# Four edits to a state-space scan that runs beside an attention layer: engine order, pairs of tokens, pairs of channels, and one broadcast load per unit

## The chip, the cores and the metric

The kernel runs on one core of a Trainium2 chip. A core has a matrix engine (PE, with its weight loads shown as PEld), a vector engine (DVE), an activation engine (ACT), a general engine (POOL) and a queue engine (SP) that here issues all the transfers. Sixteen DMA engines move the data. Work tiles lie in SBUF (128 partitions); PE writes to PSUM. Each engine runs its own list of instructions in order and waits on semaphores for the others.

The metric is device microseconds of one execution. Before the change the median of three runs was 19929.43 us (19923.0 to 19977.06).

## The reference

A batch of 16 images of 256 channels and 1024 tokens goes through two residual layers. The first is group norm, attention with 4 heads, and a feed-forward block. The second is group norm and a selective state-space scan with 512 channels `d` and 64 states `n`. The scan is what matters here:

```
delta = softplus(dt @ dt_proj_w.T + dt_proj_b)
A = -exp(A_log)

def step(h, inp):
    d_t, B_t, C_t, u_t = inp
    dA = exp(d_t[..., None] * A)
    h = dA * h + (d_t * u_t)[..., None] * B_t[:, None, :]
    y = einsum('bdn,bn->bd', h, C_t)
    return (h, y)

y = ys.transpose(1, 0, 2) + u * D
y = y * silu(z)
return (y @ out_proj_w.T) * ctx
```

For every image there are 512 x 64 recurrences over 1024 tokens, and each token's 64 states are then multiplied by `C` and summed.

## The kernel before

**Units.** The scan is cut into 4096 units: 16 images (`b`), 4 blocks of 128 channels (`k`), 4 blocks of 256 tokens (`t`), 2 halves of the channel block (`h`), 8 units (`i`) in a half. A unit holds 8 channels: each of its four scans carries two channels (`j`), 64 states each, on 128 partitions, for 256 tokens. The four scans of a unit are numbered by `r` and `e`.

**One unit's path.**
- `load` (L668) has SP bring delta times u of the 8 channels from the DRAM tile `dus` into a buffer `dub` of 128 partitions by 4 x 256 (L695): two transfers of 256 KB, each a row of 4 KB copied to 64 partitions. There are five such buffers (`dutp`, L84), and a unit's load stands in the text four units ahead.
- `inputs` (L700) multiplies the buffer by `B` on POOL, in two instructions (L705).
- `decay` (L707) spreads delta, kept as three bf16 pieces, over the partitions with four matmuls into two PSUM tiles `a` of four (L715), and ACT takes the exponential in place, four instructions (L721).
- `scan` (L723) runs four scans on DVE (L733) into `hbuf`, one buffer for each half.

`load` for the first unit of a token block also brings `pieces`, `bt` and `ct` (L674 to L682); at (h, i) = (1, 4) it brings `u_y` and `z_y`.

**Outputs of a half.** When the eight units of a half are scanned, the generator `outputs` (L749) goes on beside the next half, one `next` per unit. `sums(s)` (L755) forms the products by `C` for 32 tokens: 32 matmuls, each with a 16-column stationary piece of `cd` (the spread `C`, made by `spread_c`, L739) and a 32-column moving piece of `hbuf` (32 slots at one token), in four column groups of PE. Two ACT instructions (L774) sort the result into `y2`, eight matmuls (L780) turn it so that channels lie on partitions, and DVE adds `u * D` (L785); after the second half it multiplies by the gate (L789) and the result is stored.

**Side work.** While an image is scanned, `attention_layer` and `scan_inputs` prepare the next one and `gate_and_store` finishes the previous one. These are generators with 296 and 15 steps, fed into the loop at an even rate, 311 steps over 234 units (L806 to L842). `scan_inputs` stores delta times u into `dus` with eight transfers per block of channels (L611) and the three pieces into `dps` with two (L625).

**Who sets the order.** The text is written in the order of the main loop: `load(n + 4)`, `inputs(n + 2)`, a step of the running outputs, side steps, `scan(n)`, `decay(n + 2)`. A list scheduler of the framework then orders each engine's instructions, by its own estimate of when each could start; it may move an instruction ahead of others in the text.

Of the kernel before, what the change touches and what calls it, by code (L numbers as in the profile page):

```python
# [51 lines left out]
def attention_then_scan_kernel(  # L52
# [25 lines left out]
    wts = pool("wts", 1)  # L78
    wide = pool("wide", 8)
    half = pool("half", 4)  # L80
    pcp = pool("pcp", 2)
    ptp = pool("ptp", 4)
    small = pool("small", 2)
    dutp = pool("dutp", 5)  # L84
# [44 lines left out]

    a_neg = work("a_neg", ND * NS)
    nc.scalar.activation(a_neg, col("A_log", 0, ND * NS), AF.Exp)
    nc.vector.tensor_scalar(a_neg, a_neg, -1.0, None, ALU.mult)
    acol = const.tile([P, DI // 2], F32, name="acol")
    for k in range(ND):
        ps = psum("acol_ps")
        for j in range(2):
            nc.tensor.matmul(
                ps[ts(j, NS), :64], a_neg[:, ts(k, NS)], ident[:, j:P:2], start=True, stop=True  # L140
            )
        nc.scalar.copy(acol[:, ts(k, 64)], ps[:, :64])
    pick = const.tile([96, 16, 2, NS], BF16, name="pick")
    for p in range(3):
        r = ts(p, 32)
        v = ident[r, r].rearrange("p (i j) -> p i j", j=2)
        nc.vector.tensor_copy(pick[r], v.unsqueeze(3).to_broadcast([32, 16, 2, NS]))


    par = const.tile([P, 2], F32, name="par")  # L150
    turn = const.tile([P, 32], F32, name="turn")
    grid = ident.rearrange("p (g r) -> p g r", g=4)
    for j in range(2):
        nc.vector.tensor_reduce(par[:, j : j + 1], grid[:, :, j:16:2], AX.XY, ALU.add)
    nc.vector.tensor_tensor(
        turn.rearrange("p (g c) -> p g c", g=4), grid[:, :, 0:16:2], grid[:, :, 1:16:2], ALU.add
    )

    rel = dram1.tile([C, L], F32, name="rel", tag="rel")
    for k in range(KC):  # L160
# [301 lines left out]
    def scan_inputs(b):  # L462
# [110 lines left out]

        dps = dram.tile([ND * 3 * P, L], BF16, name="dps", tag="dps")
        dus = dram.tile([ND * NT * P, TB], F32, name="dus", tag="dus")
        dpv = dps.rearrange("(k p q) t -> k q p t", p=3, q=P)
        duv = dus.rearrange("(k t h m r) c -> k h r m t c", k=ND, t=NT, h=2, r=4)
        for d in range(ND):
            delta = work("delta")
            pss = []  # L580
            for hf in range(2):
                ps = psum("d_ps")
                nc.tensor.matmul(ps, wdt_s[:, ts(d, P)], dt[:RANK, hs(hf)], start=True, stop=True)
                pss.append(ps)
            yield
            es = [hwork("sp_e") for _ in range(2)]
            for e, ps in zip(es, pss):
                nc.scalar.activation(e, ps, AF.Abs, bias=col("dt_b", d))
                nc.scalar.activation(e, e, AF.Exp, scale=-1.0)
                nc.scalar.activation(ps, ps, AF.Relu, bias=col("dt_b", d))  # L590
            yield
            ss = [hwork("sp_s") for _ in range(2)]
            for s, e in zip(ss, es):
                nc.vector.tensor_scalar(s, e, 1.0, None, ALU.add)
                nc.vector.scalar_tensor_tensor(e, s, 1.0, e, ALU.subtract, ALU.subtract)
            yield
            for s in ss:
                nc.scalar.activation(s, s, AF.Ln)
            yield
            for hf in range(2):  # L600
                nc.vector.tensor_tensor(ss[hf], ss[hf], es[hf], ALU.subtract)
                nc.vector.tensor_tensor(delta[:, hs(hf)], ss[hf], pss[hf], ALU.add)
                yield
            del es, ss, pss
            du = work("du")
            nc.vector.tensor_tensor(du, delta, us[d], ALU.mult)
            yield
            for hh in range(2):
                for r in range(4):
                    at = 64 * hh + 16 * r  # L610
                    nc.sync.dma_start(  # L611
                        duv[d, hh, r], du[at : at + 16].rearrange("m (t c) -> m t c", t=NT)
                    )
            for hf in range(2):
                pc = pcp.tile([P, 3, HL], BF16, name="pc", tag="pc")
                o = delta[:, hs(hf)]
                nc.scalar.copy(pc[:, 0, :], o)
                yield
                nc.vector.tensor_tensor(o, o, pc[:, 0, :], ALU.subtract)
                yield  # L620
                nc.scalar.copy(pc[:, 1, :], o)
                yield
                nc.vector.tensor_tensor(pc[:, 2, :], o, pc[:, 1, :], ALU.subtract)
                yield
                nc.sync.dma_start(dpv[d][:, :, hs(hf)], pc)  # L625
        st.update(zs=zs, gs=gs, ud=ud, rows=rows, dps=dps, dus=dus)
        st["ys"] = dram.tile([DI, L], F32, name="ys", tag="ys")
        yield
# [39 lines left out]
    def load(n):  # L668
        b, k, t, h, i = units[n]
        st = state[b]  # L670
        if (h, i) == (0, 0):
            pieces = blk.tile([96, ND, TB], BF16, name="pieces", tag="pieces")
            for p in range(3):
                nc.sync.dma_start(  # L674
                    pieces[ts(p, 32)],
                    st["dps"][ds((3 * k + p) * P, P), ts(t, TB)].rearrange("(r q) t -> q r t", q=32),
                )
            bt = blk.tile([P, TB], F32, name="bt", tag="bt")
            ct = blk.tile([P, TB], F32, name="ct", tag="ct")
            for j in range(2):  # L680
                nc.sync.dma_start(bt[ts(j, NS)], st["rows"][:NS, ts(t, TB)])
                nc.sync.dma_start(ct[ts(j, NS)], st["rows"][NS:, ts(t, TB)])  # L682
            blocks[b, k, t] = {"pieces": pieces, "bt": bt, "ct": ct}
        if (h, i) == (1, 4):
# [3 lines left out]
            nc.sync.dma_start(z, st["zs"][ts(k, P), ts(t, TB)])  # L688
            blocks[b, k, t].update(u=u, z=z)
        du = dutp.tile([P, 4, TB], F32, name="dub", tag="dub")  # L690
        src = st["dus"].rearrange(
            "(k t h i j r) c -> k t h i j (r c)", k=ND, t=NT, h=2, i=8, j=2
        )[k, t, h, i]
        for j in range(2):
            nc.sync.dma_start(  # L695
                du[ts(j, NS)].rearrange("p r c -> p (r c)"), src[j : j + 1].partition_broadcast(NS)
            )
        loaded[n] = du

    def inputs(n):  # L700
# [6 lines left out]
    def decay(n):  # L707
# [3 lines left out]
        for r in range(2):  # L711
            a = aps.tile([P, 2, TB], F32, name="a", tag="a")
            for e in range(2):
                w = pick[:, 8 * e + i].rearrange("p j n -> p (j n)")
                nc.tensor.matmul(a[:, e, :], w, pieces[:, 2 * h + r, :], start=True, stop=True)  # L715
            decays[n].append(a)
        for r in range(2):
            for e in range(2):
                q = 64 * k + 32 * h + 16 * r + 8 * e + i
                a = decays[n][r][:, e, :]  # L720
                nc.scalar.activation(a, a, AF.Exp, scale=acol[:, q : q + 1])  # L721

    def scan(n):  # L723
# [3 lines left out]
        hbuf = now["h", h]  # L727
        for r in range(2):
            for e in range(2):
                s = 16 * r + 8 * e + i  # L730
                hh = hbuf[:, s, :]
                first = hbuf[:, s, TB - 1 : TB] if t else 0.0
                nc.vector.tensor_tensor_scan(  # L733
# [2 lines left out]
        del decays[n], loaded[n]  # L736


    def spread_c(b, k, t):  # L739
        if (k, t) == (0, 0):  # L740
            now["cd"] = hst.tile([P, TB // 8, P], F32, name="cd", tag="cd")
            nc.gpsimd.memset(now["cd"], 0.0)
        cd = now["cd"]
        ct = blocks[b, k, t]["ct"].rearrange("p (a c) -> p a c", c=8)
        for j in range(2):
            nc.scalar.copy(cd[ts(j, NS), :, j : j + 127 : 18], ct[ts(j, NS)])


    def outputs(b, k, t, h):  # L749
        if (t, h) == (0, 0):  # L750
            now["yb"] = yps.tile([P, HL], F32, name="yb", tag="yb")
            nc.vector.memset(now["yb"][:, :TB], 0.0)
        cd, yb, hbuf = now["cd"], now["yb"], now["h", h]

        def sums(s):  # L755
            for c in range(8):
                for g in range(4):
                    at = 32 * s + 8 * g + c
                    nc.tensor.matmul(  # L759
                        yb[32 * g : 32 * g + 16, ts(s, SLOTS)],  # L760
                        cd[:, at // 8, ts(at % 8, 16)], hbuf[:, :, at],
                        start=(c == 0), stop=(c == 7),
                    )

        for s in range(5):
            sums(s)
            yield
        sums(5)
        sums(6)
        yield  # L770
        sums(7)
        y2 = blk.tile([P, 2 * TB], F32, name="y2", tag="y2")
        for j in range(2):
            nc.scalar.activation(  # L774
                y2[:, j : 2 * TB : 2], yb[:, :TB], AF.Identity, scale=par[:, j : j + 1]
            )
        yield
        own = ts(h, 64)
        for s in range(8):
            nc.tensor.matmul(  # L780
                yb[own, ds(TB + 32 * s, 32)], y2[:, ts(s, 64)], turn, start=True, stop=True
            )
        yield
        u, z = blocks[b, k, t]["u"], blocks[b, k, t]["z"]
        nc.vector.scalar_tensor_tensor(  # L785
            u[own], u[own], col("D", k)[own], yb[own, TB:], ALU.mult, ALU.add
        )
        if h == 1:
            nc.vector.tensor_tensor(u, u, z, ALU.mult)  # L789
# [16 lines left out]
    for n, (b, k, t, h, i) in enumerate(units):  # L806
# [21 lines left out]
        if i == 0 and n > 0:  # L828
            g = outputs(*units[n - 1][:4])
            next(g)  # L830
            running.append(g)
        if (h, i) == (0, 7):
            spread_c(b, k, t)
        if at >= 12:
            due += rate
# [10 lines left out]
        pass  # L846
    for _ in gate_and_store(B - 1):
        pass


# [53 lines left out]
```

## Time and profile before

| | |
|---|---|
| median of 3 runs | 19929.43 us |
| the profiled execution | 19887.59 us |
| its span on the core | 19885.7 us |
| first scan starts, last scan ends | 474.8 us, 19855.4 us |
| DVE busy | 13669.1 us (69%) |
| PE busy | 13574.2 us (68%) |
| POOL busy | 10583.8 us (53%) |
| ACT busy | 10128.3 us (51%) |
| moved by DMA | 2845.56 MB, mean 143 GB/s |
| of that, the `dub` loads | 8192 transfers of 256 KB |

No engine is busy for more than seven tenths of the span, and the busy shares stay much the same from one image to the next. The rows of a profile give, for each group of instructions, the busy time, the mean of one, the idle time of the engine just before them and what ended most of that idle time. DVE and PE work on the scan and on the side work alike, so their sums mix two things; the last image is scanned with nothing left to prepare and shows the scan almost alone.

### The profile page before, as it was taken

The numbers are of one execution on the slowest core, as the hardware profiler recorded it, in microseconds if no ns is written. First come the engines' busy times: TensorE is split into PE (matmuls) and PEld (weight loads), VectorE is DVE, ScalarE is ACT, GpSimd is POOL, SyncE is SP. The second block draws the span as 40 slices with busy tenths as digits, with TensorE's granted clock in tenths as the row PEclk, the third lists the DMA queues.
The fourth block names the chain that finished last, engine by engine and source line by source line (L and its number), as shares of the span: only waits on it lengthen the run. The fifth ranks groups of instructions, "written<-read, shape, count | busy, mean of one in ns | idle before, by whom it ended". The sixth has DMA issues, their size and how long they took to land. (4 is left out here: it accounts for less than half of the span.)

```text
span 19885.7 us, 697095 instructions
## 1 busy us (share of the span) xinstructions
PE 13574.2 (68%) x300176; PEld 8113.6 (41%) x300176; DVE 13669.1 (69%) x20751; ACT 10128.3 (51%) x21923; POOL 10583.8 (53%) x8214
## 2 busy tenths in 40 slices
PE   6866858668586675857758677585765858668555
PEld 2433434344343443434434344343443434434333
DVE  4766767667677676766767767676676767767666
ACT  3554545545455454554545545454554555545544
POOL 0555555555555555555555555555555555555555
PEclk7876868778687786877868778687876868778666
DMA  2555555555555555555555555555555555555555
GB/s 66 134 138 148 148 147 143 141 147 150 145 142 143 144 146 156 143 140 143 149 152 143 142 143 150 148 152 134 143 147 146 151 140 147 147 145 150 147 145 140
DMA packets 1178858, 2845.56 MB, mean 143 GB/s; under 512 B 193872, under 2 KB 571088, under 8 KB 1175760
## 3 DMA queue, kind: packets, MB, share of 16 engines
q1 hardware_dynamic: 1175760, 2800.95, 52.7%
q8 instruction: 2347, 38.45, 0.9%
q14 instruction: 751, 6.15, 0.1%
HBM read 2539.08 MB, written 261.10 MB: 141 GB/s over the span
## 5 line engine op out<-in xcount | busy, mean ns | idle before, releaser
L705 POOL TENSOR_TENSOR dub<-dub,bt 128x512 f32<-128x512 f32 x8192 | 10527.2, 1311 | 8992.9 <-DMA dub<-dus 7682.3
L721 ACT ACTIVATE a<-a,acol 128x256 f32<-128x256 f32 x16384 | 6984.7, 450 | 7445.7 <-PE a L715 7166.1
L733 DVE TENSOR_TENSOR_SCAN h<-a,h,dub 128x256 f32<-128x256 f32 x12288 | 8104.6, 726 | 1151.0 <-issue 610.2
L759 PE MATMUL yb<-h,cd 128*16 128x32 f32 x262144 | 4642.6, 234 | 2477.5 <-issue 2188.6
L715 PE MATMUL a<-pieces,pick 96*128 96x256 bf16 x16384 | 3819.6, 338 | 2960.0 <-DVE h L733 2885.2
L759 PEld LDWEIGHTS yb<-h,cd 128*16 128x16 f32 x262144 | 3925.7, 115 | 3615.6 <-issue 3239.2
L715 PEld LDWEIGHTS <-pick 96*128 96x128 bf16 x16384 | 1563.1, 111 | 5561.8 <-issue 5071.8
L733 DVE TENSOR_TENSOR_SCAN h<-a,dub 128x256 f32<-128x256 f32 x4096 | 2457.2, 666 | 571.5 <-POOL dub L705 342.7
L785 DVE SCALAR_TENSOR_TENSOR u_y<-u_y,vec,yb 64x256 f32<-64x256 f32 x512 | 244.6, 478 | 2211.5 <-PE yb L780 1167.2
L354 PE MATMUL s_ps<-ka,qa 32*128 32x512 f32 x2048 | 1177.8, 917 | 64.8 <-DVE mx L345 60.7
L345 DVE TENSOR_REDUCE mx<-s_ps 128x1 f32<-128x512 f32 x1024 | 664.4, 676 | 514.5 <-PE s_ps L354 511.1
L399 ACT ACTIVATE pt<-st_ps 128x512 f32<-128x512 f32 x1024 | 563.6, 597 | 721.3 <-PE st_ps L397 719.8
L780 PE MATMUL yb<-turn,y 128*64 128x32 f32 x8192 | 691.0, 242 | 269.9 <-ACT y L774 265.7
L780 PEld LDWEIGHTS yb<-turn,y 128*64 128x64 f32 x8192 | 619.6, 158 | 466.2 <-ACT y L774 351.3
L384 PE MATMUL av<-pt,vv 128*64 128x512 f32 x2048 | 701.4, 634 | 98.0 <-ACT pt L399 97.8
L774 ACT ACTIVATE y<-yb,par 128x256 f32<-128x256 f32 x1024 | 467.6, 493 | 530.3 <-PE yb L759 523.3
L397 PE MATMUL st_ps<-qa,ka 33*128 33x512 f32 x2048 | 663.3, 649 | 0.5 <-ACT qa L374 0.5
L354 PEld LDWEIGHTS s_ps<-ka,qa 32*128 32x128 f32 x2048 | 361.9, 251 | 361.6 <-DVE mx L345 291.4
L512 PE MATMUL g_ps<-w,xp 128*128 128x256 f32 x1536 | 419.9, 420 | 0.0
L512 PEld LDWEIGHTS g_ps<-w,xp 128*128 128x128 f32 x1536 | 374.6, 328 | 15.5 <-issue 5.6
L545 DVE SCALAR_TENSOR_TENSOR u<-up,cwh,u 128x1024 f32<-128x1024 f32 x192 | 326.7, 1703 | 31.6 <-ACT u L538 30.2
L397 PEld LDWEIGHTS st_ps<-qa,ka 33*128 33x128 f32 x2048 | 176.2, 187 | 404.3 <-issue 398.5
(126 smaller groups left out, 8106.3 us busy)
## 6 DMA issues: line engine op xcount, KB each, us to landing
dub<-dus SPq DMA_DIRECT2D x8192, 256.0 KB
dps<-pc SPq DMA_DIRECT2D x128, 384.0 KB
pieces<-dps SPq DMA_DIRECT2D x768, 64.0 KB
xs<-in_x_dram SPq DMA_DIRECT2D x64, 512.0 KB
zs<-z SPq DMA_DIRECT2D x64, 512.0 KB
z_y<-zs SPq DMA_DIRECT2D x256, 128.0 KB
ud<-u SPq DMA_DIRECT2D x64, 512.0 KB
u_y<-ud SPq DMA_DIRECT2D x256, 128.0 KB
```

The lines of the kernel that those rows point to most:

```text
L345: nc.vector.tensor_reduce(mx[:, e, c, hf : hf + 1], s, AX.X, ALU.max)
L354: nc.tensor.matmul(s, qa[r, ts(c, P)], ka[r, hs(hf)], start=True, stop=True)
L384: nc.tensor.matmul(av[ts(e, 2 * DH)], vv[j // (NJ // 2)][:, j % (NJ // 2), 2 * pair + e, :], pts[e], start=(j == 0), stop=(j == NJ - 1),)
L397: nc.tensor.matmul(s, ka[r, ts(j, P)], qa[r, hs(hf)], start=True, stop=True)
L399: nc.scalar.activation(pt, s, AF.Exp)
L512: nc.tensor.matmul(ps[:, ts(q, C)], xp[k][:, ds(first + t, P, 4)], wg_s[:, k, t, :], start=(i == 0), stop=(i == 3 * KC - 1),)
L705: nc.gpsimd.tensor_tensor(v, v, bt, ALU.mult)
L715: nc.tensor.matmul(a[:, e, :], w, pieces[:, 2 * h + r, :], start=True, stop=True)
L721: nc.scalar.activation(a, a, AF.Exp, scale=acol[:, q : q + 1])
L733: nc.vector.tensor_tensor_scan(hh, decays[n][r][:, e, :], loaded[n][:, 2 * r + e, :], first, ALU.mult, ALU.add)
L759: nc.tensor.matmul(yb[32 * g : 32 * g + 16, ts(s, SLOTS)], cd[:, at // 8, ts(at % 8, 16)], hbuf[:, :, at], start=(c == 0), stop=(c == 7),)
L780: nc.tensor.matmul(yb[own, ds(TB + 32 * s, 32)], y2[:, ts(s, 64)], turn, start=True, stop=True)
```

## The change

- **Order.** At the end of the text, every instruction of PE, ACT, DVE and POOL is made to follow the one before it on its engine in the text, for the scheduler only (no semaphore comes of it). SP is not among the four.
- **Two tokens at once.** A product by `C` takes `hbuf[:, :, at : at + 2]`, 64 moving columns. `sums` has 16 matmuls instead of 32. The stationary pieces of `cd` give four rows for each of 4 pairs of tokens in place of two rows for each of 8 tokens, and half of what a matmul writes is not wanted. One ACT copy takes the 512 columns to `y2`, and 32 turning matmuls, in pairs that add into PSUM, pick the wanted rows by four masks (`turn`, 128 x 4 x 32). The steps of `outputs` are spread differently: two `sums` in each of the first four, then the turn, then DVE. `spread_c` is called at (h, i) = (0, 5) instead of (0, 7).
- **Pairs 32 apart.** The two channels of one scan are 32 apart instead of neighbours, and slots are numbered 4 i + 2 r + e. The columns of `acol`, the masks `pick` and the layouts of `dps` and `dus` follow. `dus` is stored with one transfer per block of channels instead of eight, `dps` with eight of 16 partitions by 3 x 2 KB instead of two of 128 by 3 x 1 KB, `pieces` loaded with one instead of three. `pcp` has one buffer of double length.
- **One load.** A unit's `dub` comes with one transfer of 512 KB: two rows of 4 KB, each copied to 64 partitions.

```
-    pcp = pool("pcp", 2)
+    pcp = pool("pcp", 1)
...
-    par = const.tile([P, 2], F32, name="par")
-    turn = const.tile([P, 32], F32, name="turn")
+    turn = const.tile([P, 4, 32], F32, name="turn")
+    nc.vector.memset(turn, 0.0)
     grid = ident.rearrange("p (g r) -> p g r", g=4)
...
+    for e in range(2):
+        for j in range(2):
+            v = turn[:, 2 * e + j].rearrange("p (g c e) -> p g c e", g=4, e=2)[:, :, :, e]
+            nc.vector.tensor_copy(v, grid[:, :, 2 * e + j : 16 : 4])
...
-        dpv = dps.rearrange("(k p q) t -> k q p t", p=3, q=P)
-        duv = dus.rearrange("(k t h m r) c -> k h r m t c", k=ND, t=NT, h=2, r=4)
+        dpv = dps.rearrange("(k p j s h q) t -> k h j q s p t", k=ND, p=3, j=2, h=2, q=2)
+        duv = dus.rearrange("(k t d) c -> k d t c", k=ND, t=NT)
...
-            for hh in range(2):
-                for r in range(4):
-                    at = 64 * hh + 16 * r
-                    nc.sync.dma_start(
-                        duv[d, hh, r], du[at : at + 16].rearrange("m (t c) -> m t c", t=NT)
-                    )
+            nc.sync.dma_start(duv[d], du.rearrange("d (t c) -> d t c", t=NT))
...
+            for i in range(8):
+                h, j, q = i // 4, i // 2 % 2, i % 2
+                nc.sync.dma_start(dpv[d, h, j, q], pc[ts(i, 16)])
...
-            for p in range(3):
-                nc.sync.dma_start(
-                    pieces[ts(p, 32)],
-                    st["dps"][ds((3 * k + p) * P, P), ts(t, TB)].rearrange("(r q) t -> q r t", q=32),
-                )
+            nc.sync.dma_start(
+                pieces,
+                st["dps"][ts(k, 3 * P), ts(t, TB)].rearrange("(p q) t -> p q t", q=4),
+            )
...
-        src = st["dus"].rearrange(
-            "(k t h i j r) c -> k t h i j (r c)", k=ND, t=NT, h=2, i=8, j=2
-        )[k, t, h, i]
-        for j in range(2):
-            nc.sync.dma_start(
-                du[ts(j, NS)].rearrange("p r c -> p (r c)"), src[j : j + 1].partition_broadcast(NS)
-            )
+        src = st["dus"][ts(k * NT + t, P)].rearrange(
+            "(h j i r) c -> h i j (r c)", h=2, j=2, i=8
+        )[h, i]
+        nc.sync.dma_start(
+            du.rearrange("p r c -> p (r c)"),
+            src.unsqueeze(1).to_broadcast([2, NS, 4 * TB]),
+        )
...
         def sums(s):
-            for c in range(8):
+            for c in range(4):
                 for g in range(4):
-                    at = 32 * s + 8 * g + c
+                    at = 32 * s + 8 * g + 2 * c
                     nc.tensor.matmul(
-                        yb[32 * g : 32 * g + 16, ts(s, SLOTS)],
-                        cd[:, at // 8, ts(at % 8, 16)], hbuf[:, :, at],
-                        start=(c == 0), stop=(c == 7),
+                        yb[32 * g : 32 * g + 16, ts(s, 2 * SLOTS)],
+                        cd[:, at // 8, ts(c, 16)], hbuf[:, :, at : at + 2],
+                        start=(c == 0), stop=(c == 3),
                     )
-        for s in range(5):
+        for s in range(0, 8, 2):
             sums(s)
-            yield
-        sums(5)
-        sums(6)
-        yield
-        sums(7)
+            sums(s + 1)
+            if s < 6:
+                yield
         y2 = blk.tile([P, 2 * TB], F32, name="y2", tag="y2")
-        for j in range(2):
-            nc.scalar.activation(
-                y2[:, j : 2 * TB : 2], yb[:, :TB], AF.Identity, scale=par[:, j : j + 1]
-            )
+        nc.scalar.copy(y2, yb)
+        yield
+        for s in range(8):
+            for e in range(2):
+                for j in range(2):
+                    nc.tensor.matmul(
+                        yb[64 * h + 32 * j : 64 * h + 32 * j + 32, ts(s, 32)],
+                        y2[:, 64 * s + e : 64 * s + 64 : 2], turn[:, 2 * e + j],
+                        start=(e == 0), stop=(e == 1),
+                    )
...
-        if (h, i) == (0, 7):
+        if (h, i) == (0, 5):
             spread_c(b, k, t)
...
+    last = {}
+    order = mybir.DependencyInfo(mybir.DependencyClass.NoSync, mybir.DependencyReason.DATA)
+    queues = (
+        mybir.EngineType.PE, mybir.EngineType.Activation,
+        mybir.EngineType.DVE, mybir.EngineType.Pool,
+    )
+    for ins in list(nc.cur_bb.bb.instructions):
+        if ins.engine in queues:
+            if ins.engine in last:
+                tc.add_manual_dep(ins, last[ins.engine], order, reason="program order")
+            last[ins.engine] = ins.name
```

In the instructions that come of it, the old load reads a pattern of 64 copies of a row (counts 64, 1024) and writes 64 partitions (64, 1024). The new one reads (2, 64, 1024), the 64 with a step of zero, and writes (128, 1, 1024).

## The prediction

> **What bounds the kernel now.** I read the groups of instructions first, then the busy times by stretch, the timeline of one half, SP's waits, and the queues.
>
> ```profile
> L705 POOL TENSOR_TENSOR dub<-dub,bt 128x512 f32<-128x512 f32 x8192 | 10527.2, 1311 | 8992.9 <-DMA dub<-dus 7682.3
> L721 ACT ACTIVATE a<-a,acol 128x256 f32<-128x256 f32 x16384 | 6984.7, 450 | 7445.7 <-PE a L715 7166.1
> L733 DVE TENSOR_TENSOR_SCAN h<-a,h,dub 128x256 f32<-128x256 f32 x12288 | 8104.6, 726 | 1151.0 <-issue 610.2
> L759 PE MATMUL yb<-h,cd 128*16 128x32 f32 x262144 | 4642.6, 234 | 2477.5 <-issue 2188.6
> L785 DVE SCALAR_TENSOR_TENSOR u_y<-u_y,vec,yb 64x256 f32<-64x256 f32 x512 | 244.6, 478 | 2211.5 <-PE yb L780 1167.2
> ...
> ```
>
> Every engine waits for another one. The largest single wait of DVE, the busiest, is L785: 2211.5 us over 512 instructions, for the outputs of a half.
>
> ```profile
> 5367.00:6591.00 1224.00, 844.61 (x18671) 507.12 (x18671) 850.27 (x1296) 631.43 (x1370) 663.94 (x513) 0.77 0.54 145
> 18790.00:19855.00 1065.00, 594.41 (x17970) 407.05 (x17973) 678.56 (x1076) 483.48 (x1107) 637.17 (x509) 0.68 0.56 145
> ```
>
> Columns: the stretch, its length, busy time (and instructions) of PE, PEld, DVE, ACT, POOL, then clock, DMA share, GB/s. One middle image takes 1224 us, of which DVE works 850; the last, with hardly any side work, takes 1065, of which DVE works 679. So 370 to 390 us of an image are waits, with side work or without.
>
> ```profile
> 19319.41 0.58 PE L715 MATMUL a<-pieces,pick 96*128 96x256 bf16 x2 [0.70 <-DVE h L733]
> 19319.92 2.17 PE L759 MATMUL yb<-h,cd 128*16 128x32 f32 x137
> 19323.37 2.01 PE L759 MATMUL yb<-h,cd 128*16 128x32 f32 x128 [1.28 <-issue]
> 19327.94 0.33 PE L759 MATMUL yb<-h,cd 128*16 128x32 f32 x9 [2.56 <-issue]
> 19328.20 0.39 PE L715 MATMUL a<-pieces,pick 96*128 96x256 bf16 x2
> ```
>
> The cause: PE has a whole half's products in one block, and the next decay (L715) waits 8.8 us behind them. 128 products take 2.01 us, then PE stands still with nothing to wait for that the profile shows: 3.45 us for 128, 27 ns each.
>
> **The load, which decides.** These rows price it.
>
> ```profile
> SPq L695 <- DVE h L733: 11439.4, 3554, 30.9
> ...
> q1 hardware_dynamic: 1175760, 2800.95, 52.7%
> ...
> 5415.00:5420.00 5.00, 1.62 (x11) 1.15 (x12) 3.33 (x6) 1.03 (x3) 0.00 (x0) 0.50 1.03 415
> 16415.00:16420.00 5.00, 0.79 (x3) 0.10 (x1) 5.00 (x10) 1.81 (x5) 0.00 (x0) 0.50 1.03 419
> ```
>
> Today SP waits for a free buffer (11439.4 us), not for the engines of the transfers, which are 52.7% busy. In the two fullest stretches share 1.03 goes with 415 and 419 GB/s: a DMA engine moves at most 419/16 = 26.2 GB/s. The packet records agree: a 4 KB packet takes 159 ns in the fastest quarter (25.8 GB/s), 239 ns on average. Today's two transfers make 128 packets a unit, 8 per engine.
>
> The new transfer moves the same 128 packets. Its cost hangs on how many engines share them, and no row shows a transfer of this form. Near end: all 16, 8 x 159 ns = 1.3 us of each engine, as now. Far end: an engine for each of its two source rows, 64 x 159 ns = 10.2 us per unit, and 64 x 239 ns = 15.3 us with the mean packet. I take the far end with the fast packet. Every transfer of the program before, whatever its size, has the same first count on both sides, 16, 32, 64 or 128, which cuts into 16 shares along the first dimension. The new one reads (2, 64, 1024) and writes (128, 1, 1024): along the first dimension of both sides it can only be cut in two, and its nearest relative, the 64-row load of before, was cut along its 64. The fast packet, because it is what the full queue of the two stretches shows, and two busy engines crowd each other less than sixteen. `pieces` (384 rows read, 96 written) still cuts into 16, `dus` (128) and `dps` (16) too; these I leave at their old cost.
>
> [...]
>
> At the far end the two engines bound everything. Of five buffers (L84) one is being scanned and one is with POOL, so about three loads always queue, and none of the unit's other work reaches 10.2 us: POOL 2 x 1.31, ACT 4 x 0.45, DVE 4 x 0.73 to 4.9 with its waits. The sum against the profiled span of 19885.7 us:
>
> - until the first scan, 475 us (474.8 now);
> - 4096 units x 64 packets x 159 ns = 41,680 us;
> - the two engines' part of all other transfers: 2801 - 2147 = 653 MB over 16 engines, at 26.2 GB/s 1,560 us; at the mean of the queue's row (52.7% of 19886 = 10,480 us per engine, less 32,768 dub packets x 239 ns) 2,650 us. I take 2,150;
> - the outputs and last steps after the last scan, 30 us.
>
> Together 44,340 us. Side loads issued behind three dub loads arrive 30 us later than now, but a unit takes as long as its load, so DVE and the loads wait for the same queue; I add 60 us. Forecast 44,400 us. Bounds: 4096 x 512 KB at 2 x 26.2 GB/s + 1,560 + 505 = 43,050 below; 4096 x 15.3 + 2,650 + 505 = 65,800 above.
>
> **The other parts**, which this hides. What covers them is the 10.2 us per unit; without that cover they give the second case.
>
> - Order and products. The 64 passes of a unit's products (two per matmul, as 262144 rows for 131072 matmuls show) stand after its predecessor's decay, four units out of eight. Price of one 64-column pass: not below the 14 ns at which 32-column ones follow each other inside a burst (2.01 us / 128 = 15.7), not above twice that. So 0.9 to 2.0 us, plus the decays 4 x 0.2, under the 2.58 us of four back-to-back scans (660 us of scans per image / 256). The turn grows from 8192 to 32768 passes; at 58 ns in one column group or 29 in two that is 1.9 to 3.7 us in the fifth unit. ACT loses 1024 x 493 ns and gains 512 copies of some 0.6 us: 200 us less, off the path. L785 then waits no longer: 2211 us back.
> - Side steps now keep their place: 311 in 234 units, so 77 units hold two, and the second usually needs the first from PE or ACT. PE gets to it after the decay (0.6) and products (0 to 1.7), takes 1 to 3 us (a step of L512 is 12 passes that start 234 ns apart); ACT after its exponentials (0.6 + 0.9). DVE then stands about 2 us: 155 us per image.
> - SP: 4096 loads fewer x 0.53 us, 448 `dus` and 512 `pieces` fewer, 384 `dps` more. SP has 11,439 us of waiting to absorb any of it. One `pcp` buffer makes a block's split wait for its store; blocks come ten units apart. POOL's clearing of `cd` shrinks from 4096 to 2560 columns, 16 times.
>
> **Rivals.**
>
> - *Sixteen engines after all: faster.* Speaks for it: same bytes, same packets. Against: the counts. Then 475 + 15 x (850 + 155) + 679 + 10 + 30 = 16,270 us; with 60 to 250 us of side stalls per image 14,850 to 17,700. It decides from where a unit's load takes less than a unit: at 1220/256 = 4.8 us per unit the kernel stands where it was, that is from five engines on (128/5 x 159 ns = 4.1 us).
> - *Two engines, other two each time.* Several loads then run side by side; one buffer's round is 0.5 issue + 10.4 + 2 to land + 2.6 POOL + 2.6 scan = 18 us, over five buffers 3.6 us per unit, 256 x 3.6 = 925 us per image, hidden under 1005 in part: with some 140 us of it showing, about 18,500 us. Against: nothing in the instruction names engines, and each has the same form.
> - *Sixteen engines, but the fixed order costs more than the burst did.* If each of 311 steps stalls DVE 1.5 us: 475 + 15 x (850 + 467) + 719 = 20,950 us. It turns the sign from 1.2 us per step (370/311). Against: in a unit with one step the result is a unit old.
> - *The order doesn't hold.* The built program's PE, ACT, DVE and POOL do follow the text; no chance kept.
>
> **How the numbers follow.** Two engines, the same ones: 0.80. Sixteen, faster: 0.12. Two changing ones: 0.04, faster. Sixteen with a slow order: 0.03, slower. The rest, 0.01, lies within 0.3%, about what a measurement of this kernel can tell from no change. So faster 0.16, same 0.01, slower 0.83. The range must leave out the 0.20 of the other cases, so it is the likeliest one's own: from its lower bound, 43,000, to 58,000, where the packet would take 215 ns; I leave 215 to 239 out, since the mean comes from crowded engines.
>
> **What would show it.** Right: the DMA share of 16 engines falls to about 2/16 plus a little (some 15 to 20%) while the rate falls to about 65 GB/s; POOL L705 waits for `dub<-dus` more than 30,000 us; the landing of a load takes 20 to 40 us; a middle image takes about 2,750 us, the last almost as long; L785 no longer among DVE's waits. Wrong: a rate above 150 GB/s, a load landing within 6 us, units at 2.6 us in the last image. Then the second case holds, and its own test is idle time of DVE before side lines in units that hold two steps.

## The result and the profile after

The changed kernel takes 44515.32 us in the median of four runs (44506.89 to 44522.89), beside 19949.06 us (19923.0 to 19977.06) for the kernel before: 2.231 times as long, 95% interval 2.228 to 2.235. The prediction was 44,400 us. The profiled execution has a span of 44504.4 us.

First the busy times, the DMA totals, the row of the queue that carries the transfers, and the chain of work that ended last, by engine and by line.

```profile
PE 15716.7 (35%) x193680; PEld 8657.2 (19%) x193680; DVE 13643.5 (31%) x20753; ACT 10263.6 (23%) x21285; POOL 10215.5 (23%) x8214
...
DMA packets 1021264, 2830.65 MB, mean 64 GB/s; under 512 B 61776, under 2 KB 389840, under 8 KB 1019088
...
q1 hardware_dynamic: 1019088, 2800.42, 16.9%
...
DMA 88%; SPq 6%; POOL 2%; DVE 2%; PE 1%; issue 1%; ACT 0%; POOLq 0%; DVEq 0%; ACTq 0%
DMA dub<-dus 85%; POOL dub L702 2%; SPq L691 2%; DVE h L730 1%; DMA ys<-u_y 1%; SPq L679 1%; SPq L684 1%; DMA xs<-in_x_dram 1%; SPq L678 1%; DMA y<-ys 1%; SPq L671 0%; SPq L685 0%; SPq L790 0%; SPq L634 0%; SPq L180 0%
```

DVE's work is what it was (13,644 us against 13,669), but it is now 31% of the span. The queue moves the same 2800 MB and is busy for 16.9% of 16 engines, that is 2.7 engines, and the load of `dub` alone is 85% of the chain. A low DMA share does not say here that DMA has room to spare: it is a mean over sixteen engines, and most of them stand idle (for 86% of the span exactly two packets of the queue are in flight).

The groups of POOL's product with `B` and of the scans:

```profile
L702 POOL TENSOR_TENSOR dub<-dub,bt 128x512 f32<-128x512 f32 x8192 | 10180.0, 1264 | 34252.1 <-DMA dub<-dus 34177.3
...
L730 DVE TENSOR_TENSOR_SCAN h<-a,h,dub 128x256 f32<-128x256 f32 x12288 | 8215.9, 731 | 21266.9 <-POOL dub L702 21248.5
...
```

And, in another view, the line that takes a half's outputs:

```profile
L785 DVE SCALAR_TENSOR_TENSOR u_y<-u_y,vec,yb 64x256 f32<-64x256 f32 x512 | 239.3, 467 | 16.0 <-PE yb L777 7.8
```

POOL's waits (total, times, longest):

```profile
POOL dub L702 <- DMA dub<-dus: 34177.3, 4089, 463.6
...
```

And a stretch of one image's length from the middle of the run, with the columns of the prediction's table of stretches:

```profile
19900.00:22657.00 2757.00, 980.90 (x12104) 541.39 (x12104) 851.79 (x1296) 641.19 (x1330) 637.89 (x513) 0.55 0.17 64
```

POOL waits for the load in 4089 of 4096 units, 8.4 us each, and DVE's scans wait for POOL. An image is 2757 us long, though DVE still works 852 us in it as before. The timeline of one unit (start, length, engine and line, in brackets the idle time before) shows the chain as it repeats:

```profile
20017.18 2.49 POOL L702 TENSOR_TENSOR dub<-dub,bt 128x512 f32<-128x512 f32 x2 [8.74 <-DMA dub<-dus]
...
20020.03 2.67 DVE L730 TENSOR_TENSOR_SCAN h<-a,h,dub 128x256 f32<-128x256 f32 x4
...
20023.27 1.91 PE L760 MATMUL yb<-h,cd 128*16 128x64 f32 x64
...
20030.73 2.48 POOL L702 TENSOR_TENSOR dub<-dub,bt 128x512 f32<-128x512 f32 x2 [11.06 <-DMA dub<-dus]
20032.03 2.67 DVE L730 TENSOR_TENSOR_SCAN h<-a,h,dub 128x256 f32<-128x256 f32 x4 [9.33 <-POOL dub L702]
```

Each unit has its 2.5 us on POOL and its 2.7 us on DVE, and then both stand idle for 9 to 11 us here. Over the whole trace a unit takes 10.73 us: 43,941 us from the start of the first scan (528 us) to the end of the last (44,470 us), over 4096.

### The profile page after: what moved, and what is told of

Its sections match the earlier page's. It is cut to its first block, busy times and chain, and to the rows that moved or that the text cites. A ratio compares the mean times of both kernels' runs of the same rounds, so it can differ in the third digit from the quotient of the medians.

```text
span 44504.4 us, 472521 instructions
## 1 busy us (share of the span) xinstructions
PE 15716.7 (35%) x193680; PEld 8657.2 (19%) x193680; DVE 13643.5 (31%) x20753; ACT 10263.6 (23%) x21285; POOL 10215.5 (23%) x8214
## 2 busy tenths in 40 slices
DMA packets 1021264, 2830.65 MB, mean 64 GB/s; under 512 B 61776, under 2 KB 389840, under 8 KB 1019088
## 3 DMA queue, kind: packets, MB, share of 16 engines
q1 hardware_dynamic: 1019088, 2800.42, 16.9%
## 4 chain that ended last, share of the span: by engine, by line
DMA 88%; SPq 6%; POOL 2%; DVE 2%; PE 1%; issue 1%; ACT 0%; POOLq 0%; DVEq 0%; ACTq 0%
DMA dub<-dus 85%; POOL dub L702 2%; SPq L691 2%; DVE h L730 1%; DMA ys<-u_y 1%; SPq L679 1%; SPq L684 1%; DMA xs<-in_x_dram 1%; SPq L678 1%; DMA y<-ys 1%; SPq L671 0%; SPq L685 0%; SPq L790 0%; SPq L634 0%; SPq L180 0%
## 5 line engine op out<-in xcount | busy, mean ns | idle before, releaser
L702 POOL TENSOR_TENSOR dub<-dub,bt 128x512 f32<-128x512 f32 x8192 | 10180.0, 1264 | 34252.1 <-DMA dub<-dus 34177.3
L712 PE MATMUL a<-pieces,pick 96*128 96x256 bf16 x16384 | 4684.8, 389 | 27736.2 <-DVE h L730 27359.0
L712 PEld LDWEIGHTS <-pick 96*128 96x128 bf16 x16384 | 1924.8, 118 | 31339.4 <-issue 30647.1
L760 PE MATMUL yb<-h,cd 128*16 128x64 f32 x131072 | 3847.4, 304 | 26.0 <-DVE h L730 19.6
L760 PEld LDWEIGHTS yb<-h,cd 128*16 128x16 f32 x131072 | 3308.9, 138 | 843.1 <-issue 726.4
L777 PE MATMUL yb<-turn,y 128*32 128x32 f32 x32768 | 981.4, 241 | 0.7 <-ACT y L772 0.7
L777 PEld LDWEIGHTS yb<-turn,y 128*32 128x32 f32 x32768 | 912.9, 156 | 206.6 <-ACT a L718 195.1
L645 PE MATMUL m_ps<-w,y 128*128 128x256 f32 x1024 | 398.5, 549 | 475.6 <-DMA y<-ys 475.1
L494 PE MATMUL z_ps<-xp,w 128*128 128x512 f32 x512 | 411.9, 953 | 6.7 <-DVE xp L481 6.7
L533 PE MATMUL u_ps<-xp,w 128*128 128x512 f32 x512 | 407.4, 943 | 5.1 <-ACT u L539 5.1
```

The lines of the kernel that those rows point to most:

```text
L702: nc.gpsimd.tensor_tensor(v, v, bt, ALU.mult)
L712: nc.tensor.matmul(a[:, e, :], w, pieces[:, 2 * h + i // 4, :], start=True, stop=True)
L760: nc.tensor.matmul(yb[32 * g : 32 * g + 16, ts(s, 2 * SLOTS)], cd[:, at // 8, ts(c, 16)], hbuf[:, :, at : at + 2], start=(c == 0), stop=(c ...
L777: nc.tensor.matmul(yb[64 * h + 32 * j : 64 * h + 32 * j + 32, ts(s, 32)], y2[:, 64 * s + e : 64 * s + 64 : 2], turn[:, 2 * e + j], start=( ...
```

## The experiments

Times are medians; a ratio is to the kernel before on the same chip.

**1. The load alone, undone and done.** The changed kernel with two loads of 64 copies again, and the kernel before with the one load:

```
 (changed kernel)
-        nc.sync.dma_start(
-            du.rearrange("p r c -> p (r c)"),
-            src.unsqueeze(1).to_broadcast([2, NS, 4 * TB]),
-        )
+        for j in range(2):
+            nc.sync.dma_start(
+                du[ts(j, NS)].rearrange("p r c -> p (r c)"), src[j : j + 1].partition_broadcast(NS)
+            )
 (kernel before: the same edit the other way round)
```

> The changed kernel with the unit's load as two transfers of 64 copies again (counts 64 and 64), all else kept. Theory 1 (the merged transfer is shared by two engines and bounds everything): 16,270 us by the second case of the prediction, 14,850 to 17,700. Theory 2 (the text order or the products of two tokens make the units slow, the load only shows it): stays above 40,000 us. Theory 3 (sixteen engines, but the fixed order stalls every step): about 20,950 us.

> The kernel before with nothing changed but the load: one transfer of 512 KB whose source counts are (2, 64, 1024). Theory 1: the load alone makes the change's time: 4096 units x (64 packets x 160 ns + 0.5 us for the other transfers' share) + 475 + 30 = 44,500 us, 44,000 to 45,500. Theory 2: stays near 19,930 us.

With two loads: 17552.01 us (17492.3 to 17564.85), ratio 0.881, interval 0.879 to 0.883. The kernel before with the one load: 44618.43 us, one run. So the form of the load alone makes the loss, in either kernel, and the other three edits together make a gain. The DMA totals, of the two loads first and then of the kernel before with one load, show how:

```profile
DMA packets 1144228, 2831.83 MB, mean 162 GB/s; under 512 B 184656, under 2 KB 512720, under 8 KB 1141968
```

```profile
DMA packets 1055897, 2844.40 MB, mean 64 GB/s; under 512 B 70992, under 2 KB 448208, under 8 KB 1052880
```

The packets under 512 B give the number of engines, if a transfer leaves one of them on each engine that shares it; the two packets that are in flight for 86% of the span say the same of the changed kernel. From two loads to one the changed kernel loses 184,656 - 61,776 = 122,880 of them, and 8192 transfers on 16 engines less 4096 transfers on 2 are 131,072 - 8,192 = 122,880, exactly. (In the records they are 4 bytes each. The kernel before issues 12,117 transfers in all, and 16 x 12,117 is its 193,872, so each of its transfers leaves sixteen.) The kernel before loses the same 122,880 by the same edit (193,872 of its own to 70,992).

**2. The dose.** Two loads as above, but each reads its row as 4 times 16, or as 8 times 8 copies, so that the first count is 4 or 8 (the edit for 4):

```
-                du[ts(j, NS)].rearrange("p r c -> p (r c)"), src[j : j + 1].partition_broadcast(NS)
+                du[ts(j, NS)].rearrange("p r c -> p (r c)"),
+                src[j : j + 1].unsqueeze(1).to_broadcast([1, 4, 4 * TB]).unsqueeze(2).to_broadcast([1, 4, NS // 4, 4 * TB])[0],
```

> As e1_two_loads, but each of the two transfers reads its row as 4 x 16 copies (counts 4, 16, 1024 against 64). Bytes, packets and number of transfers are those of e1. Theory 1, with the first count deciding: 4 engines, 32 packets each per unit, 32 x 160 ns + 0.5 us = 5.6 us per unit, 4096 x 5.6 + 570 = 23,600 us. Rival (being one transfer per unit is what costs, not the counts): as e1. Rival (each transfer takes other engines than the one before): as e1 or some per cent above.

> As e3_four_shares with 8 x 8 copies (counts 8, 8, 1024). Theory 1: 8 engines, 16 packets each, 16 x 160 ns + 0.5 us = 3.1 us per unit, less than a unit takes for its other work, so within 3% of e1_two_loads. Rival (any inner dimension of step zero is slow): as far above e1 as e3.

Measured: 23884.74 us with 4 and 18069.59 us with 8, one run each, both as expected (the second 2.9% above the two plain loads, where 3% was allowed). The DMA totals of the two:

```profile
DMA packets 1045924, 2831.44 MB, mean 119 GB/s; under 512 B 86352, under 2 KB 414416, under 8 KB 1043664
```

```profile
DMA packets 1078692, 2831.57 MB, mean 157 GB/s; under 512 B 119120, under 2 KB 447184, under 8 KB 1076432
```

184,656 - 86,352 = 98,304 is 8192 x 12, and 184,656 - 119,120 = 65,536 is 8192 x 8: four and eight engines. The bytes and the 4 KB packets are the same in all of these; with a first count of the source of 2, 4, 8 and 64 they are shared by 2, 4, 8 and 16 engines, and the changed kernel takes 44,515, 23,885, 18,070 and 17,552 us.

**3. What the other edits are worth.** Four kernels with two loads: the kernel before with nothing but the order of the text; the changed kernel without it; and the changed kernel with the products, sorting and turn of before on the new layout, without the order and (further down) with it.

```
 (order: the block at the end of the text, added to the kernel before or taken out)
 (old products on the new layout, its core)
-                        yb[32 * g : 32 * g + 16, ts(s, 2 * SLOTS)],
-                        cd[:, at // 8, ts(c, 16)], hbuf[:, :, at : at + 2],
-                        start=(c == 0), stop=(c == 3),
+                        yb[32 * g : 32 * g + 16, ts(s, SLOTS)],
+                        cd[:, at // 8, ts(at % 8, 16)], hbuf[:, :, at],
+                        start=(c == 0), stop=(c == 7),
...
+                y2.rearrange("p (s j x) -> p j s x", j=2, x=SLOTS)[:, :, j],
```

> The kernel before, with nothing but the order of the text on PE, ACT, DVE and POOL. Theory A (the order takes the 8.8 us blocks of products apart, and the 2211 us at the DVE line of the outputs go with them): 512 passes of a half stand 64 to a unit, at 27 ns 1.7 us beside 2.6 us of scans; only the sixth unit holds 128. So 17,500 to 18,300 us, close to the 17,552 us of the changed kernel with two loads. Theory B (what helps there is that half as many passes are made): no gain, 19,600 to 20,500 us, with PE behind in each unit. Theory C (the gain came from fewer and longer transfers of dus, dps and pieces): no gain either, 19,900 us, and the DVE line of the outputs keeps its wait only if the order doesn't hold.

> The changed kernel with two loads and without the order of the text. Theory A: the products stand in one block again, with half the passes (256 and 64 of the turn, at 17 to 27 ns 5.5 to 8.6 us against 16 before), so about half of the gain is gone: 18,500 to 19,800 us, and the wait before the DVE line of the outputs is back at 1,000 us or more. Theory B (halved passes): 17,400 to 17,800 us, as with the order. Theory C (transfers): 17,400 to 17,800 us too; B and C part by the run of the kernel before with the order alone, and by whether DVE's wait for the outputs is short here.

> The changed kernel with two loads and without the order, and with the products, the sorting and the turn of before on the new layout; what is left of the change is the pairs 32 apart and their transfers. Theory B (the 2,440 us by which the kernel without the order stands below the kernel before come from halving the passes of the products): back to 19,500 to 20,100 us, with some 2,200 us at the DVE line of the outputs. Theory C (they come from the fewer transfers of dus, dps and pieces): 17,300 to 17,700 us.

Measured: the kernel before with the order 17999.08 us, ratio 0.904 (0.902 to 0.905), inside theory A's range. The changed kernel without the order 17474.6 us, ratio 0.878 (0.877 to 0.880), so not slower than the 0.881 (0.879 to 0.883) with it: A's 18,500 to 19,800 us fails there, and the number is B's. With the old products and no order 19768.68 us, ratio 0.991 (0.990 to 0.993): the pairs and their transfers are worth some 170 us, and halving the passes, without the order, some 2,290. (Halving the passes stands here and below for the whole edit of two tokens at once, with its sorting, its turn and its place of `spread_c`; these were not taken apart.) Theory C falls.

A's wait was there all the same. The group of the line that takes a half's outputs (busy, mean of one, idle before it), in four kernels: before with the order; changed, two loads, with the order; the same without the order; old products without the order.

```profile
L785 DVE SCALAR_TENSOR_TENSOR u_y<-u_y,vec,yb 64x256 f32<-64x256 f32 x512 | 242.3, 473 | 259.6 <-PE yb L780 181.6 <-ACT a L721 65.6 <-ACT sp_e L588 3.5
```

```profile
L785 DVE SCALAR_TENSOR_TENSOR u_y<-u_y,vec,yb 64x256 f32<-64x256 f32 x512 | 241.4, 471 | 183.8 <-PE yb L777 132.9 <-issue 22.1 <-ACT a L718 21.8
```

```profile
L785 DVE SCALAR_TENSOR_TENSOR u_y<-u_y,vec,yb 64x256 f32<-64x256 f32 x512 | 241.7, 472 | 1497.0 <-PE yb L777 925.8 <-ACT a L718 295.8 <-issue 234.6
```

```profile
L786 DVE SCALAR_TENSOR_TENSOR u_y<-u_y,vec,yb 64x256 f32<-64x256 f32 x512 | 243.6, 476 | 1997.8 <-PE yb L781 1143.5 <-ACT a L719 535.4 <-issue 314.5
```

With the order the wait is 260 us with the old products and 184 us with halved passes; without it 1,998 us and 1,497 us. Where the halved passes stand without the order can be seen on PE in the last image:

```profile
17009.41 0.59 PE L712 MATMUL a<-pieces,pick 96*128 96x256 bf16 x2 [0.70 <-DVE h L730]
17009.93 4.67 PE L760 MATMUL yb<-h,cd 128*16 128x64 f32 x167
17014.89 0.40 PE L760 MATMUL yb<-h,cd 128*16 128x64 f32 x11 [0.28 <-issue]
17015.22 0.39 PE L712 MATMUL a<-pieces,pick 96*128 96x256 bf16 x2
```

The products are still one block, of which 178 passes stand ahead of the next decay, 5.3 us (17009.93 to 17015.22). In the kernel before it was 274 passes and 8.3 us (19319.92 to 19328.20 in the prediction's timeline, whose 8.8 us begin with the decay ahead of them). So the order does take the block apart. Why it is worth nothing there, a sum over all of DVE's groups shows, idle time in us after the first scan:

| | before scans | before the outputs' line | before other lines |
|---|---|---|---|
| before | 1,714 | 2,212 | 1,995 |
| before, with the order | 1,202 | 260 | 2,379 |
| changed, two loads, old products, no order | 1,531 | 1,998 | 2,262 |
| changed, two loads, no order | 769 | 1,497 | 1,185 |
| changed, two loads | 953 | 184 | 2,305 |

From the third row to the fourth, halving the passes saves 501 us before the outputs' line, but 762 us before the scans and 1,077 us before the side lines: it is not the block of the outputs alone that it helps. From the fourth row to the fifth the order wins 1,313 us at the outputs and gives 1,120 us back before the side lines and 184 us before the scans. The sums differ by 9 us. Without the order the scheduler has moved the side lines: the 64 instructions of L518, for one, stand 12 scans, three units, earlier in the median. That this is why DVE waits less there fits, but was not tested by itself.

**4. Where the order holds, the place in the text decides.** The side steps of a unit go behind its scans, then half of them between two pairs of scans, then (scans first) with six buffers for the loads, one unit earlier, and last (scans first) without the order:

```
 (changed kernel with two loads; scans first)
+        scan(n)
         if at >= 12:
             due += rate
             while due >= 1.0:
                 next(side, None)
                 due -= 1.0
-        scan(n)
 (scans in halves)
+        for r in range(2):
+            scan(n, r)
+            if at >= 12:
+                due += rate / 2
...
 (six buffers)
-    dutp = pool("dutp", 5)
+    dutp = pool("dutp", 6)
-    AHEAD = 4
+    AHEAD = 5
```

> The changed kernel with two loads, and a unit's side steps behind its scans in the text, not ahead of them. Theory S (in the kernel with two loads some 2,100 us of DVE's waits stand before side lines because DVE comes to the step while PE still has the decay and the products in front of it; a unit's scans, 2.6 us, cover that): 100 us less in each of 15 images, 16,000 us (15,700 to 16,600). Rival (the waits are the chain inside a unit that holds two steps, or loads that come late): 17,300 to 17,700 us, nothing gained.

> As the run before, but a unit's four scans are two pairs, with side steps due behind each pair, so that two steps of one unit stand 1.3 us of scans apart. Theory S with units of two steps as the rest of the stall: 200 to 500 us below the run with the scans first. Rival (what is left there is not in the double units, or 1.3 us is too short for PE's or ACT's answer): within 150 us of it, or above.

> The run with the scans first, with six buffers for the loads of delta u instead of five and loads five units ahead. Theory (what still holds DVE before its scans, 645 us put down to POOL and behind it the loads, comes from loads that stand on SP behind transfers that wait for DVE, so that they go out too late; one unit more of lead, some 3.8 us, covers most of them, of which the longest is about 20 us): 300 to 600 us less, 15,500 to 15,800 us. Rival (the loads then come early, but POOL stands at the scans' own pace, or the side loads are pushed back by as much): within 100 us of 16,100 us.

> The run with the scans first, without the order of the text. Theory (the scheduler's own order holds the outputs back as one block wherever the text puts the steps, and moves the side steps as it likes, so that what the text says of them is lost without the order): 17,200 to 17,700 us, as the other run without the order, with more than 1,000 us at the DVE line of the outputs. Rival (the place in the text helps by itself): 16,000 to 16,600 us.

Scans first: 16102.75 us, ratio 0.809 (0.808 to 0.810), as theory S had it. One side step in both kernels, with the steps first and with the scans first, in the timeline:

```profile
5933.19 0.60 PE L712 MATMUL a<-pieces,pick 96*128 96x256 bf16 x4
...
5933.72 1.09 PE L760 MATMUL yb<-h,cd 128*16 128x64 f32 x64
...
5934.75 2.24 PE L645 MATMUL m_ps<-w,y 128*128 128x256 f32 x8
...
5937.03 0.69 DVE L651 SCALAR_TENSOR_TENSOR xs<-xs,m_ps 128x512 f32<-128x512 f32 x1 [3.65 <-PE m_ps L645]
```

```profile
5470.56 5.24 DVE L730 TENSOR_TENSOR_SCAN h<-a,h,dub 128x256 f32<-128x256 f32 x8 [0.61 <-POOL dub L702]
...
5471.32 2.24 PE L645 MATMUL m_ps<-w,y 128*128 128x256 f32 x8
...
5475.71 0.67 DVE L651 SCALAR_TENSOR_TENSOR xs<-xs,m_ps 128x512 f32<-128x512 f32 x1
```

In the first, DVE has finished its scans and waits 3.65 us while PE does the decay (0.6), the products (1.09) and only then the step's own 2.24 us. In the second, the same 2.24 us of PE lie under the scans, and L651 starts without a wait. DVE's waits before side lines fall from 2,305 to 808 us; those before the scans stay (1,022).

Scans in halves: 16222.74 us, 0.815 (0.814 to 0.817), slower than scans first; that units of two steps are the rest of the stall is refuted in this form. Most of the 120 us that it costs stand before side lines, where DVE waits 915 us in place of 808; why was not followed up. Six buffers: 16087.77 us, 0.808 (0.805 to 0.810), no different from five. DVE's wait for POOL, with five buffers and then with six, hardly moved,

```profile
DVE h L730 <- POOL dub L702: 644.9, 315, 10.5
```

```profile
DVE h L730 <- POOL dub L702: 620.6, 271, 11.6
```

so an earlier load is not what is missing. Scans first without the order: 17443.26 us, 0.876 (0.875 to 0.878), with 1,533 us at the outputs' line: without the order the place in the text is lost. The new place is worth 1,449 us with the order (17,552 to 16,103) and 31 us without it (17,475 to 17,443).

> The run before this one, with the order of the text and a unit's scans ahead of its side steps: what the halved passes are worth where nothing stands in blocks. PE then has 64 passes a unit at 27 ns, 1.7 us, in place of some 1.1 to 1.9 us. If the products are hidden under the scans there: 16,100 to 16,400 us, like the run with scans first. If PE's answers to the side steps still come later by the longer products (as 17,999 against 17,552 us with the steps first): 16,400 to 16,900 us.

That one, scans first with the order and the old products, takes 16513.27 us, 0.829 (0.827 to 0.830): the halved passes are worth 410 us there, not 2,290. The number lies in the second range expected, but not for the reason given: DVE's waits before side lines are the same (801 and 808 us), and what the old products add stands before the scans (1,350 us in place of 1,022) and the outputs' line (328 in place of 193).

The fastest of this study are the changed kernel with two loads and the scans ahead of the side steps, with five buffers or six, at 0.81 of the time before.

## Why the prediction was right

**The engines.** The step that decided, two engines for the new load because its first count is 2, held, in its reason too: the same edit gives 44,618 us in the kernel before, and with two loads the first count of the source alone moves the time, from 23,885 us on 4 engines to 18,070 on 8 and 17,552 on 16. The counts of small packets agree at 2, 4 and 8 with 16 as the base. That `pieces`, `dus` and `dps` still go to sixteen held as well: the changed kernel issues 7,445 transfers, and its 61,776 small packets less 2 for each of the 4096 loads are 53,584, 16 for each of the other 3,349. Merging a unit's two loads into one, in this form, cost a factor of 2.5 (44,515 against 17,552 us), because it put a count of 2 first.

**Always the same two.** That the two are the same for every unit was an estimate in the prediction; no row of before shows it. Of the rivals, two changing engines had about 18,500 us; the time excludes them. The packet records say the same from their side: two packets in flight for 86% of the span, though about three loads stand in the queue (31.6 us in the median from the start of a load's issue to POOL's start, at 10.7 us a unit).

**The sum.** Its terms against the trace: the start 528 us, not 475. (The 474.8 and 19,855.4 us given for the kernel before are 11.5 us too late when counted from the span's start: its first scan starts at 463.3 us and its last ends at 19,843.8.) A packet of 4 KB: 159 ns was taken; the some 482,000 of them that ran with one or two others took 161.9 ns in the mean, so 262,144 x 161.9 = 42,440 us, not 41,680. What is left of the 43,941 us of scanning for all other transfers and delays is then 1,500 us, not 2,210; this is a difference, not a measurement. The end 35 us, not 30. The two larger misses, +760 and -710, cancel by luck. The packet lies inside its bounds, 159 and 239 ns; the other transfers lie below theirs, 1,560 and 2,650 us, if only a little, since 32 MB of them move before the first scan or after the last. So the fast rate was right for both terms, and the middle value taken for the second was too high. That two engines crowd each other less than sixteen agrees with the mean 4 KB packet, 166 ns against 239 in the kernel before, but the two full stretches have all sixteen at work and packets of 161 and 159 ns. The range's upper end, 58,000 us, was far; it stands for a packet of 211 ns by the sum's own terms, not 215.

**The signs named.** DMA share 15 to 20%: 16.9% on the queue. Rate about 65 GB/s: 64. POOL waiting more than 30,000 us for the load: 34,177. A load's landing 20 to 40 us: from the end of its issue to POOL's start 23.8 us in the median. A middle image 2,750 us, the last almost as long: 2,757 and 2,663. L785 gone from DVE's waits: 16 us of idle time before it.

**The cover.** That the long load hides all other edits is shown by the kernel before with the one load: only 103 us separate it (one run) from the changed kernel.

**The second case, which two loads bring about,** had 16,270 us (14,850 to 17,700); 17,552 us is near its upper end. Its term for side steps, 15 x 155 = 2,325 us, was right: 2,305. The wait at the outputs does go, but for 184 us. Mis-sized was the rest: it counted no waits before the scans, and there were 953 us; with the 184 that is 1,137 of the 1,282 us missing. The break-even from five engines on agrees with 23,885 us at four and 18,070 at eight.

The price of a pass was read from two rows as "3.45 us for 128, 27 ns each", but those 3.45 us hold the 137 passes of the first row, 25 ns each; with the next row and both pauses it is 265 passes in 8.02 us, 30 ns each. Nothing in the forecast rests on it.

What that case did not see is which edit carries it. It gave 2,211 us to order and products together. Each alone brings most of the gain (1,915 us by the order in the kernel before, 2,290 by the halved passes without it), and the two do not add. It also took the side waits as a price that the order adds, and as fixed. The kernel before already had 1,995 us of them, and with the scans ahead of the steps 808 us are left.

**Left open:** what the 1,022 us before the scans of the fastest kernel go back to (645 of them end with POOL's product, and an earlier load did not shorten these), and why the scans in halves lose. That each step stalls 1.5 us, the rival with a slow order, did not come up in any run.

## What to carry to other kernels

Before two transfers are merged into one, look at the first count of the source: here a broadcast whose source had 2, 4 or 8 as its first count ran on 2, 4 or 8 DMA engines (44,515, 23,885 and 18,070 us), and the count of the smallest packets showed it. A DMA share of 17% was here a queue at its limit, with two packets in flight for 86% of the span. Where a fixed order and a smaller burst remove the same wait, measure each alone, since they don't add; and once the order holds, put the work that needs another engine's answer behind work that doesn't.

## What the runs showed of the hardware

- **The mean packet was longer where the loads went to more engines.** 4 KB packets take 166 ns in the mean when the loads go to two engines, 170 with four, 217 with eight, 237 with sixteen, while the fastest quarter takes 159 ns or less in all of them. Sixteen busy engines alone do not make it so: in the two full stretches of the prediction, with a share of 1.03, the 4 KB packets took 161 and 159 ns in the mean. What does make it so was not found. Going from eight engines to sixteen won 3% of the time; at eight a unit's 16 packets of 217 ns, 3.5 us, already lie below the 4.2 us that a unit takes with sixteen (1,085 us a middle image, over 256).
- **The granted clock of PE was lower in the changed kernel than with two loads.** It is 0.55 in the one and 0.73 in the other, for the same 193,680 matmul instructions, whose busy time is 15,717 us (35% of the span) in the one and 12,143 us (69%) in the other. What sets the clock was not found. PE is 1% of the changed kernel's chain, so its clock does not show in the time there.
- **Passes followed each other faster than one is recorded to last.** One pass of 64 columns is recorded with 260 ns in the mean with two loads, but 64 of them stand in 1.09 us in the timeline above, 17 ns each. They are spread over four column groups; that the groups are the reason was not tested. In the prediction the price lay between 14 and 28 ns. In the changed kernel 64 passes stand in 1.91 us, 30 ns each, just above it, where the granted clock is 0.50 (20023.30 to 20025.10), and in 1.09 us where it is 1.00 (1089.70 to 1090.85).
